# Window attention: the writes of the q and k pieces two slots later on the DMA queue, the layouts of a unit one slot sooner

## The chip, the cores and the metric

The kernel runs on one core of a Trainium2 chip. The metric is the device time of one execution in microseconds, the median of several executions. The core has a matrix engine (TensorE, PE in the profile; its weight loads are PEld), three engines for elementwise work (VectorE or DVE, ScalarE or ACT, GpSimd or POOL), and SyncE (SP). In this kernel SP does nothing but ask for DMA transfers, one after the other, in a fixed order; a request that has to wait holds up all behind it. The row SPq of the profile is that queue.

## The reference: what is computed

The input x has 16 sequences of 512 rows of 128 numbers. The reference is one pre-norm block of attention followed by a product-key expert layer:

```python
x = x + attn(layernorm(x), w_qkv, w_proj)
x = x + ffn(layernorm(x), gamma, beta, w_q, keys, key_in, key_out)
```

Only the attention matters for this change:

```python
q, k, v = split(einsum('btc,oc->bto', x, w_qkv), 3)   # 16 heads of 8 numbers each
attn = einsum('bhqd,bhkd->bhqk', q, k) / sqrt(8)
attn = where(abs(i - j) > 128, -1e9, attn)            # a window of 128 to either side
out  = einsum('bhqk,bhkd->bhqd', softmax(attn), v)
return einsum('btc,oc->bto', out, w_proj)
```

## The kernel before

The program has two stages. The first is the attention for all 16 sequences, with the second norm running beside it; the second stage is the expert layer, which starts when the attention is over. The change touches the first stage alone.

**Units and slots.** A sequence b has 16 heads; four heads together (a group g) make a *unit*, n = 4b + g, so there are 64 units. A unit has four *slots*, u = 0 to 3, one for each block of 128 rows. One loop over s = 4n + u writes out the work of every slot by hand: the scores of unit n + 2 (`greatest`, PE into `s_ps`, then a maximum on DVE into `mx`), the exponentials of unit n (`exponentials`, PE into `e_ps`, then ACT into `pT`, POOL cutting the window), the product with v of two slots earlier (`weigh`), and at most one step of work that is spread over the slots: `preparing` (norm, q, k and v of a sequence ahead), `ending` (the projection of the sequence behind) and `beside` (norms and the weights of the experts). PE and POOL keep the order in which the loop writes their work. The DMA requests are put into one fixed order on SP as well.

**Pieces.** The scores are computed in bf16 at fp32 accuracy: q and k of a sequence are each split into three bf16 pieces whose sum is the fp32 number. POOL does that in `prepare`, in four operations over as many slots: a copy (piece 0), a difference, a copy (piece 1), a difference (piece 2). The tile `pc` holds the three pieces (`qp` or `kp` in the profile).

**Write.** The pieces lie in SBUF with one channel per partition. The score matmul needs pieces and channels of one head together along the partitions, so the tile goes through DRAM: one DMA (L363, 384 KB) writes the three pieces to a DRAM tile `qv` or `kv`. There are 16 writes of q and 16 of k.

**Layout.** `lay(n)` reads them back in the order in which the matmuls want them, into one of six buffers `qst` and `kst`: three DMAs for q (L390), each 96 KB, where one piece is read as three broadcast copies; three for k (L390), 96 KB each; one that clears three rows (L394, `zeros`). The layout of unit n + 4 is asked for in slot 3 of unit n, so it is first read (by the scores) at the beginning of the unit after next:

```python
if u == NQ - 1 and 0 <= n + LAID < NU:
    lay(n + LAID)
```

**The rows of the maximum.** The maximum of every row, negated and split into three pieces as well, is put under q as three more rows of `qst`, so that the matmul of the exponentials subtracts it. POOL splits it in slot 0 of the next unit (`greatest_pieces`), PE transposes it and ACT copies it to `mT` in slot 1 (`greatest_rows`, L440), and three DMAs of 4 KB (L442) move it into `qst`. The first matmul `e_ps` of the following unit needs them.

**What else is asked on SP in this stage:** the load of expert weights (L191, L212), and the transposed second norm of a finished sequence (`xT`, L525, 256 KB).

**The order around the change.** SP has no slots. It asks for the next transfer as soon as that transfer's own conditions hold: its source is written, its destination is read for the last time, and the transfer eight places earlier has landed, for eight completion semaphores are used in turn. In the order before the change, a unit in which a write is asked has on SP: the three mT, the write, the seven of the layout, then the mT of the next unit. The step of `preparing` that asks for a write is in slot 3, after `greatest_rows` of slot 1 and ahead of the layout in the same slot. The q write stands in one unit of a sequence's four and the k write in the next.

In the profile, L168 is the helper for all matmuls of the first stage, L175 for its transposes and L172 for its POOL operations, and L615 is the helper of the second stage.

Of the kernel before, what the change touches and what calls it, by code (L numbers as in the profile page):

```python
# [11 lines left out]
BF16 = mybir.dt.bfloat16  # L12
# [8 lines left out]
P = 128  # L21
# [22 lines left out]
def kernel(  # L44
# [13 lines left out]
    nc = tc.nc  # L58
    B, T, D = x.shape
    NH = 16  # L60
    DK = D // NH
    NQ = T // P
# [18 lines left out]
    for b in range(B):  # L81
        t = keep.tile([P, NQ, D], F32, name=f"x_{b}")
# [59 lines left out]
    def load(b):  # L142
        xts[b] = ahead.tile([P, T], F32, tag="xt", name=f"xt_{b}")
        nc.sync.dma_start(xts[b], xT[b])
# [8 lines left out]
    with ExitStack() as at:  # L153
# [4 lines left out]
        dr = at.enter_context(tc.tile_pool(name="dr", bufs=2, space=bass.MemoryType.DRAM))  # L158
# [7 lines left out]
        def mm(*args, **kw):  # L166

            tc.keep_in_program_order(nc.tensor.matmul(*args, **kw))  # L168

        def pool(op, *args, **kw):  # L170

            tc.keep_in_program_order(getattr(nc.gpsimd, op)(*args, **kw))  # L172
# [92 lines left out]
        NU, NBUF = B * NG, 6  # L265
# [10 lines left out]
        pieced, attns, norms = {}, {}, {}  # L276
# [26 lines left out]
        def ln_stats(bs, name, into):  # L303

            n = len(bs) * NQ
            mv = ln.tile([P, n, 2], F32, tag=f"mv{name}{n}", name=f"mv{name}_{bs[0]}", bufs=3)
            for i in range(n):
                st = ln.tile([P, 6], F32, tag="st", name=f"st{name}_{bs[0]}_{i}", bufs=4)
                nc.vector.bn_stats(st, xs[bs[i // NQ]][:, i % NQ])
                nc.vector.bn_aggr(mv[:, i], st)  # L310
                if i % NQ == NQ - 1:
                    yield
            rstd = ln.tile([P, n], F32, tag=f"rs{name}{n}", name=f"rs{name}_{bs[0]}", bufs=3)
            nc.scalar.activation(rstd[:, 0:n], mv[:, 0:n, 1], AF.Sqrt, bias=eps)
            nc.vector.reciprocal(rstd[:, 0:n], rstd[:, 0:n])
            for i, b in enumerate(bs):
                into[b] = mv[:, i * NQ : i * NQ + NQ], rstd[:, i * NQ : i * NQ + NQ]
            yield

        def normalised_T(b, mv, rstd, dst, tag, then=None):  # L320

            xn = w2.tile([P, NQ, D], F32, tag="xn", name=f"{tag}_{b}")
            for t in range(NQ):

                alone = b == B - 1 if tag == "xi" else b < 2
                what = (xn[:, t], xs[b][:, t], mv[:, t, 0:1], rstd[:, t : t + 1], ALU.subtract, ALU.mult)
                if t % 2 and not alone:
                    pool("tensor_scalar", *what)
                else:
                    nc.vector.tensor_scalar(*what)  # L330
                if t % 2:
                    yield BANK if t == NQ - 1 else None
            ps = ps_m.tile([P, NQ, P], F32, tag="m", name=f"{tag}_ps_{b}")
            for t in range(NQ):
                tr(ps[:, t], xn[:, t], ident)
            nc.scalar.copy(dst, ps.rearrange("p t q -> p (t q)"))
            yield then

        def prepare(b):

            xnT = w2.tile([P, T], F32, tag="xnT", name=f"xnT_{b}")
            yield from normalised_T(b, *norms.pop(b), xnT, "xn", BANK)
            fulls = []
            for what, w in (("q", wqT), ("k", wkT)):
                ps = ps_m.tile([P, T], F32, tag="m", name=f"{what}_ps_{b}")
                mm(ps, lhsT=w, rhs=xnT, start=True, stop=True)
                full = w2.tile([P, T], F32, tag="full", name=f"{what}f_{b}")
                nc.scalar.mul(full, ps, 1.0 / math.sqrt(DK) if what == "q" else 1.0)
                fulls.append((what, full))
                if what == "q":  # L350
                    yield BANK
            for what, full in fulls:
                pc = w2.tile([P, 3, T], BF16, tag="pc", name=f"{what}p_{b}")
                rest = w2.tile([P, T], F32, tag="rest", name=f"rest_{what}_{b}")
                pool("tensor_copy", pc[:, 0], full)
                yield
                pool("tensor_tensor", rest, full, pc[:, 0], ALU.subtract)
                yield
                pool("tensor_copy", pc[:, 1], rest)
                yield  # L360
                pool("tensor_tensor", pc[:, 2], rest, pc[:, 1], ALU.subtract)
                via = dr.tile([3, P, T], BF16, tag=f"{what}v", name=f"{what}v_{b}")
                nc.sync.dma_start(via.rearrange("s c t -> c s t"), pc)  # L363
                pieced[what, b] = via
                yield BANK if what == "k" else None
            va = vaug[b % 3]
            if b < 3:
                nc.gpsimd.memset(va, 0.0)
                nc.gpsimd.memset(va[:, :, :, DK : DK + 1], 1.0)
            v_ps = ps_m.tile([P, NQ, NH, DK], F32, tag="m", name=f"v_ps_{b}")  # L370
            for t in range(NQ):
                mm(
                    v_ps[:, t].rearrange("p h k -> p (h k)"),
                    lhsT=xnT[:, t * P : (t + 1) * P], rhs=wvT, start=True, stop=True,
                )
            nc.scalar.copy(va[:, :, :, 0:DK], v_ps)
            yield

        def lay(n):
# [90 lines left out]
        def weigh(n, u):  # L470

            b, g = divmod(n, NG)
            ts = near(u)
            q0, w = ts[0] * P, len(ts) * P
            pT = probs.pop((n, u))
            if u == 0:
                outs[n] = ps_o.tile([P, T], F32, tag="o", name=f"o_ps_{n}")
            for j in range(4):
                mm(
                    outs[n][32 * j : 32 * j + 32, q0 : q0 + w], lhsT=vaug[b % 3][:, u, 4 * g + j],  # L480
                    rhs=pT[:, j, 0:w], start=u == 0, stop=u == NQ - 1, skip_group_check=True,
                )
            if u == NQ - 1:
                oT = w2.tile([P, T], F32, tag="oT", name=f"oT_{n}")
                nc.scalar.copy(oT, outs[n])
                outs[n] = oT
# [31 lines left out]
        def second_norm(bs):  # L518
            into = {}
            yield from ln_stats(bs, "b", into)  # L520
            for b in bs:
                t = w2.tile([P, T], F32, tag="xiT", name=f"xiT_{b}")
                yield from normalised_T(b, *into[b], t, "xi")
                nc.vector.bn_stats(bn_st[:, b], t)
                nc.sync.dma_start(xT[b], t)  # L525
# [4 lines left out]
        AHEAD, LAID, LATE = 2, 4, 2  # L530
# [8 lines left out]
        for s in range(-2 * NG * NQ, (NU + 1) * NQ):  # L539
            n, u = divmod(s, NQ)  # L540
            b, g = divmod(n, NG)
            if g == NG - 1 and u == 2 and b + 3 < B:
                preparing.rest()
                preparing.add(prepare(b + 3))
            if u == 0 and g == 1 and b == 0:
                beside.add(ln_stats(range(4, B), "a", norms), weights_of_experts())
            if u == 0 and g == 2 and b in groups:
                beside.add(second_norm(groups[b]))
            if u == 0 and g == 2 and b == B - 1:
                load(0)  # L550
                load(1)
            tops_of = greatest(n + AHEAD, u) if 0 <= n + AHEAD < NU else iter(())
            probs_of = exponentials(n, u) if 0 <= n < NU else iter(())
            next(tops_of, None)
            next(probs_of, None)
            next(tops_of, None)
            if 0 <= s - LATE < NU * NQ:
                weigh(*divmod(s - LATE, NQ))
            together(tops_of, probs_of)
            free = True  # L560
            if u == 0 and 0 <= n + AHEAD - 1 < NU:
                greatest_pieces(n + AHEAD - 1)
            if u == 1 and 0 <= n + AHEAD - 1 < NU:
                greatest_rows(n + AHEAD - 1)
                free = False
            if u == 2 and 0 <= n - 1 < NU:
                divide(n - 1)
                free = False
                if n % NG == 0:
                    ending.add(project(n // NG - 1))  # L570
                    ending.go(False)
            for steps in (preparing, ending, beside):
                free = steps.go(free)
            if u == NQ - 1 and 0 <= n + LAID < NU:
                lay(n + LAID)
        beside.add(second_norm([B - 1]))
        ending.rest()
# [366 lines left out]
    for i in range(NB):  # L944
        b, t = divmod(i, NQ)
# [109 lines left out]
```

## Time and profile before

| | |
|---|---|
| median of 3 runs | 1598.37 us (1592.62 to 1599.02) |
| profiled execution, its own time | 1591.23 us |
| span of the profiled execution | 1588.4 us |
| busy: PE, DVE, ACT, POOL | 90%, 86%, 76%, 69% of the span |
| PE busy, 120 to 740 us (attention) | 575 us of 620 us |
| PE busy, 765 to 1588 us (experts) | 753 us of 823 us |
| mean granted clock of PE | 0.987 |
| DMA, q1 (all that SP asks for) | 71.59 MB, 15.3% of 16 engines over the span |

How to read it: the page gives for every engine the time it was busy, and for every idle stretch which event ended it (its releaser). A line such as "PE s_ps L168 <- DMA qst<-mT" is PE standing idle ahead of a matmul that writes `s_ps`, until a transfer from `mT` into `qst` landed. Lines with SPq tell how long SP held a request, and for what. "issue" is time in which an engine waited for nothing that the profile shows. The chain of waits follows the work that ended last back from the end, so that it shows what a shorter wait could shorten. Ends of matmuls are modelled, so short gaps on PE are less certain than the long ones.

### The profile page before, as it was taken

To read this page: it belongs to the slowest core of one execution; us is meant where nothing else is said; L and a number is where in the kernel's file an instruction comes from. 1 tells how busy PE (TensorE), PEld (TensorE's weight loads), DVE (VectorE), ACT (ScalarE), POOL (GpSimd) and SP (SyncE) were. 2 spreads that over 40 slices of the span, in tenths; PEclk is the share of its full clock that TensorE was granted. 3 is DMA by queue.
4 is the path that set the end of the run, shared out by engine and by line. 5 is a ranking of instruction groups with operands and counts; after the bars stand their busy time and mean duration, and the time that the engine had idled before them with its cause. 6 is when DMAs were issued, how large, how long until landed. Compare 5 with 4: busy or idle time off the path is not lost.

```text
span 1588.4 us, 49415 instructions
## 1 busy us (share of the span) xinstructions
PE 1430.3 (90%) x16880; PEld 837.5 (53%) x16880; DVE 1363.5 (86%) x7998; ACT 1213.0 (76%) x2593; POOL 1092.8 (69%) x1706
## 2 busy tenths in 40 slices
PE   4899999999999999987689999999999999999998
PEld 1344444444444444433356666666666666666666
DVE  6787778888878887885799999999999999999994
ACT  1476676677767776677688988898988988988973
POOL 8465666666666676655377777777777777777785
PEclk9999999999999999999799999999999999999998
DMA  6233232222222233221000000000000000000000
GB/s 181 66 106 94 86 88 80 74 81 76 71 77 86 83 96 92 75 62 40 34 9 3 16 9 15 16 9 16 9 16 16 9 16 9 16 15 9 9 2 22
DMA packets 53579, 75.00 MB, mean 47 GB/s; under 512 B 5840, under 2 KB 39888, under 8 KB 53200
## 3 DMA queue, kind: packets, MB, share of 16 engines
q1 hardware_dynamic: 52496, 71.59, 15.3%
q8 instruction: 133, 2.18, 0.6%
q14 instruction: 118, 0.97, 0.2%
q10 hardware_dynamic: 832, 0.26, 0.1%
HBM read 49.28 MB, written 20.97 MB: 44 GB/s over the span
## 4 chain that ended last, share of the span: by engine, by line
PE 40%; DVE 21%; ACT 17%; DMA 9%; POOL 8%; issue 3%; SPq 2%; DVEq 0%; ACTq 0%; POOLq 0%
PE o_ps L168 7%; PE s_ps L168 7%; ACT L615 5%; PE e_ps L168 5%; DMA qst<-qv 5%; DVE idx L615 4%; PE off_ps L615 4%; PE dn_ps L615 4%; DMA qst<-mT 4%; DVE row L615 4%; PE up_ps L615 3%; DVE masked L415 3%; ACT gel L615 2%; ACT pT L457 2%; PE sim_ps L615 2%
## 5 line engine op out<-in xcount | busy, mean ns | idle before, releaser
L415 DVE CUSTOM_DVE_ANT_0 masked<-s_ps,band 128x384 bf16<-128x384 f32 (+1 forms) x1024 | 498.5, 487 | 140.4 <-PE s_ps L168 35.5
L457 ACT ACTIVATE pT<-e_ps 128x384 f32<-128x384 f32 (+1 forms) x1024 | 390.6, 436 | 172.8 <-PE e_ps L168 168.1
L172 POOL TENSOR_SCALAR_AFFINE_SELECT pT<-pT 128x512 f32<-128x512 f32 x384 | 237.8, 635 | 238.8 <-ACT pT L457 238.5
L168 PE MATMUL s_ps<-kst,qst 128*128 128x384 bf16 (+1 forms) x1024 | 313.9, 308 | 45.1 <-DVE mx L415 13.1
L615 POOL TENSOR_TENSOR cols<-mine,wT 64x512 f32<-64x512 bf16 x256 | 269.4, 1052 | 39.9 <-DVE mine L615 14.5
L615 PEld LDWEIGHTS w_ps<-cols,row 128*64 128x64 f32 x8192 | 246.8, 138 | 52.8 <-POOL cols L615 48.6
L615 PE MATMUL w_ps<-cols,row 128*64 128x32 f32 x8192 | 256.4, 223 | 9.8 <-POOL cols L615 9.6
L615 POOL TENSOR_TENSOR g<-g,gel 128x512 f32<-128x512 f32 x128 | 163.5, 1277 | 124.1 <-ACT g L615 124.1
L168 PE MATMUL e_ps<-qst,kst 128*128 128x384 bf16 (+1 forms) x1024 | 225.8, 302 | 12.0 <-DMA qst<-mT 7.8
L168 PEld LDWEIGHTS <-qst 128*128 128x128 bf16 x1024 | 100.3, 98 | 216.9 <-issue 155.9
L168 PE MATMUL o_ps<-pT,vaug 128*32 128x384 f32 (+1 forms) x2048 | 192.4, 448 | 0.4 <-POOL pT L172 0.3
L615 DVE FIND_INDEX8 idx<-top,sim 128x8 uint32<-128x32 f32 x1024 | 166.2, 185 | 0.0
L615 ACT ACTIVATE row<-off_p,one 128x512 f32<-128x512 bf16 x256 | 165.7, 747 | 0.0
L615 ACT ACT_TABLE_LOAD x122 | 156.5, 1283 | 2.2
L615 DVE TENSOR_TENSOR row<-x_ps,nums_p 128x1024 f32<-128x1024 f32 x128 | 150.1, 1214 | 0.0
L615 ACT ACTIVATE off_p<-off_ps 128x512 bf16<-128x512 f32 x256 | 133.4, 603 | 20.9 <-PE off_ps L615 20.9
L615 PE MATMUL up_ps<-g,key_out_sb 64*128 64x256 f32 (+2 forms) x1152 | 146.3, 380 | 0.0
L168 PEld LDWEIGHTS <-kst 128*128 128x128 bf16 x1024 | 97.8, 98 | 53.4 <-issue 19.5
L615 PE MATMUL dn_ps<-xt,key_inT 128*64 128x256 f32 x1024 | 125.3, 388 | 0.0
L615 PE MATMUL off_ps<-p_bf,ident_bf 128*128 128x512 bf16 x256 | 99.9, 390 | 19.9 <-ACT p_bf L615 19.5
L615 DVE MAX8 top<-sim 128x8 f32<-128x32 f32 x1024 | 106.8, 177 | 4.6 <-ACT sim L615 4.6
L615 DVE FIND_INDEX8 place<-best,cand 128x8 uint32<-128x64 f32 x512 | 101.0, 218 | 0.0
(145 smaller groups left out, 2343.4 us busy)
## 6 DMA issues: line engine op xcount, KB each, us to landing
qst<-qv SPq DMA_DIRECT2D x192, 96.0 KB
kst<-kv SPq DMA_DIRECT2D x192, 96.0 KB
qv<-qp SPq DMA_DIRECT2D x16, 384.0 KB
kv<-kp SPq DMA_DIRECT2D x16, 384.0 KB
x<-in_L_attn_x_dram SPq DMA_DIRECT2D x16, 256.0 KB
xT<-xiT SPq DMA_DIRECT2D x16, 256.0 KB
xt<-xT SPq DMA_DIRECT2D x16, 256.0 KB
out_dram<-o_sb SPq DMA_DIRECT2D x16, 256.0 KB
```

What stands on the lines that cost most here:

```text
L168: tc.keep_in_program_order(nc.tensor.matmul(*args, **kw))
L172: tc.keep_in_program_order(getattr(nc.gpsimd, op)(*args, **kw))
L415: nc.vector.tensor_tensor_reduce(masked[:, 0:w], s, band.rearrange("p u k -> p (u k)")[:, from_u : from_u + w], 1.0, LOWEST, ALU.add, ALU. ...
L457: nc.scalar.activation(pT[:, h, 0:w], e_ps[:, 0:w], AF.Exp)
L615: return lambda *args, **kw: tc.keep_in_program_order(op(*args, **kw))
```

## The change

Two things are moved, and nothing else.

The request that writes the q pieces is no longer made behind the last of the four POOL operations on q, but two slots later, behind the third POOL operation on k. The request for the k pieces is made one step of `preparing` after the v matmuls, in a new last step, which is two slots later as well. Until a write is asked for, `pieced` holds the SBUF tile; from then on the DRAM tile. The layout of unit n + 4 is asked for in slot 2 of unit n in place of slot 3.

```diff
@@ prepare(b)
+            def write(what):
+
+                via = dr.tile([3, P, T], BF16, tag=f"{what}v", name=f"{what}v_{b}")
+                nc.sync.dma_start(via.rearrange("s c t -> c s t"), pieced[what, b])
+                pieced[what, b] = via
+
             for what, full in fulls:
...
                 pool("tensor_copy", pc[:, 1], rest)
+                if what == "k":
+                    write("q")
                 yield
                 pool("tensor_tensor", pc[:, 2], rest, pc[:, 1], ALU.subtract)
-                via = dr.tile([3, P, T], BF16, tag=f"{what}v", name=f"{what}v_{b}")
-                nc.sync.dma_start(via.rearrange("s c t -> c s t"), pc)
-                pieced[what, b] = via
+                pieced[what, b] = pc
                 yield BANK if what == "k" else None
...
             nc.scalar.copy(va[:, :, :, 0:DK], v_ps)
+            yield
+            write("k")
             yield
@@ the loop over slots
-            if u == NQ - 1 and 0 <= n + LAID < NU:
+            if u == NQ - 2 and 0 <= n + LAID < NU:
                 lay(n + LAID)
```

In the order on SP this gives, in the steady part of the stage: the three mT, the write, the layout, and so on, as before; but a write stands behind the mT of the unit after the one in which it stood. The transfers of `xT` and of the expert weights that were asked between a write and a layout stand behind the layout. The orders of PE, DVE and ACT are the same in both kernels.

## The prediction

> **What bounds the kernel now.** I read the page first: PE is busy 90% of the span, and the chain that ended last gives DMA 9%: "DMA qst<-qv" 5%, "DMA qst<-mT" 4%. Both belong to the attention stage (roughly 40 to 755 us); the expert stage after it has no line of the change. So the question is what PE loses to these two transfers. The waits of PE between 120 and 740 us answer it; columns: us in total, times, longest.
>
> ```profile
> PE s_ps L168 <- DMA qst<-mT: 12.8, 13, 2.5
> PE e_ps L168 <- DMA qst<-mT: 7.8, 17, 1.3
> PE s_ps L168 <- DMA qst<-zeros: 4.1, 6, 1.8
> ```
>
> That is 24.7 us of PE standing still for rows of the maximum (mT) or the last piece of a layout (zeros). Next, why these land late: the waits of the SP queue, which asks for every transfer in turn.
>
> ```profile
> SPq L363 <- POOL qp L172: 60.9, 16, 5.2
> SPq L363 <- POOL kp L172: 43.4, 16, 4.0
> SPq L442 <- DMA qst<-qv: 12.0, 21, 1.1
> ```
>
> Each of the 32 writes (L363) holds the queue until POOL has made the last piece, 3.3 us on average (104.3/32); behind it stand the layouts and the next mT. The timeline of SP over three units shows it: after the mT of 549.03 the queue sits from 550.94 to 555.00, the layout goes out only then, and the mT of 559.89 is asked the moment the layout is through. Where no write is asked (581.90), the layout follows its mT at once.
>
> ```profile
> 549.03 1.91 SPq L442 DMA_DIRECT2D qst<-mT  x3
> 555.00 0.39 SPq L363 DMA_DIRECT2D qv<-qp  x1
> 555.44 2.21 SPq L390 DMA_DIRECT2D qst<-qv  x3
> 559.89 2.48 SPq L442 DMA_DIRECT2D qst<-mT  x3
> ...
> 581.90 1.91 SPq L442 DMA_DIRECT2D qst<-mT  x3
> 583.86 2.22 SPq L390 DMA_DIRECT2D qst<-qv  x3
> ```
>
> The chain of waits through one such place runs from POOL over the write and the layout into the mT, and then into PE (start, length):
>
> ```profile
> 521.10 1.13 POOL kp L172
> 522.25 0.39 SPq L363
> 524.58 5.75 DMA qst<-qv
> 530.35 2.27 DMA qst<-mT
> 532.71 0.38 PE e_ps L168 x2
> ```
>
> Last, the size of it: four units of one batch, cut at the copies of mT. Columns: length, then busy time of PE, PEld, DVE, ACT, POOL, granted clock, DMA share, GB/s.
>
> ```profile
> 548.45:558.47 10.02, 9.99 (x86) 5.35 (x84) 8.55 (x37) 7.41 (x21) 8.09 (x15) 1.00 0.16 49
> 558.47:570.20 11.73, 10.56 (x86) 5.30 (x84) 10.32 (x45) 7.88 (x22) 8.38 (x15) 1.00 0.33 106
> 570.20:581.30 11.10, 9.51 (x81) 4.75 (x79) 9.80 (x39) 8.01 (x21) 7.70 (x15) 1.00 0.40 120
> 581.30:591.86 10.56, 10.41 (x78) 4.73 (x78) 8.37 (x37) 7.84 (x21) 6.40 (x14) 1.00 0.26 73
> ```
>
> Call them A, B, C and D. PE is idle 0.03, 1.17, 1.59 and 0.15 us: only the two units behind a write lose anything. The same cut over the thirteen batches from 124.78 us gives an idle time of 15.8 us in the B units and 19.4 us in the C units, 35.2 in 26 units (1.35 each); it holds the 24.7 named above and the small gaps around them. Three C units (136.22, 438.38, 613.42) ran at a granted clock of 0.87 right after stalls of 1.8, 2.5 and 1.2 us: PE is busy 11.22, 10.82 and 11.32 there, against 9.9, 9.1 and 9.5 in C units like them. That is 4.8 us more that hang on the stalls.
>
> **The change part by part.** No instruction is added, removed or given another shape. The orders of PE, DVE and ACT stay as they were; POOL's differs in its first 60 instructions alone, where a half of xn comes ahead of the last k piece in place of a memset (about 0.8 us by half of the 1.59 us for two, against 0.95): startup 0, between -1 and +1 us, for the first score matmul waits on that k piece (10.24 us idle before it at 37.16). What moves is on SP.
>
> *The writes.* Before: mT, write, layout. After: mT, layout (no write any more in that gap), mT, write, layout: the same place, one unit later. The pieces of the q write at 511.59 would be asked for behind the mT of 516.46, when they have been ready for over 5 us. The 104.3 us of SP waiting go, and with them the delay of layout and mT. POOL's queue is not touched. A write costs SP 0.39 us, ahead of the layout as now.
>
> *The layouts.* Seven requests (three q, three k, one zeros; 2.21 + 1.25 + 0.77 us and gaps, 4.35 in all). In a unit without a write they leave as soon as SP has sent the mT, so an earlier slot gives them nothing; it puts them ahead of the loads of expert weights, and of anything else asked at the slot. One line has one answer: 0 by itself.
>
> *What the move puts at risk.* Eight transfers can be open: a request waits for the one eight before it. The third mT therefore waits for the second q layout, or for the third where an xT lies between. From the chain above: the second q layout lands at 530.33, 8.1 us after its write began at 522.25. In the new order the write begins some 2.0 us behind its mT (1.91 and a gap), so that layout lands 10.1 us after the first mT, and the next third mT goes out at 10.4 + 1.2 = 11.6 us: 1.5 us of margin, 0.75 with an xT (one more q request, 0.75). That is thin, and covers it all; if it is gone, the wait of today is back in the same place. The k write is laid out one unit after it is written instead of two: about 11 us against 18 (522.25 to 540.26); in the startup the layout of k followed its write within 2.8 us (27.86 to 30.63), so this costs 0.
>
> *What is late next.* Units without a trouble idle 0.15 (D); the two early units with writes and no stall (82.95 and 93.49) idle 0.75 and 0.67. I put 0.5 us of idle time on each of the 26 units, nearer to the early ones as these have the same work on SP: 35.2 - 13 = 22.2 us saved; the bounds are 35.2 - 18.2 = 17 and 35.2 - 3.9 = 31. Of the slow-clock stretches two of three go: 3 us (0 to 4.8). D now follows a write, a layout and an xT: I charge 0.2 us in each of 13: -2.6 (0 to -6). Sum 22.2 + 3 - 2.6 = 22.6. The profiled execution took 1591.23 us (span 1588.4, 2.8 around it): 1569. The median shown is 7.1 us above it, so I forecast 1575.
>
> **Rivals.**
> *The transfer engines stay full (1582).* A unit without a write has a DMA share of 0.16 over 10.02 us: 25.7 engine-us of 16 engines. The q layouts are written as three broadcast copies; if the whole layout lay on three engines they would be busy 8.6 us of it, and a write (0.33 x 16 x 11.73 - 25.7 = 36 engine-us, 2.3 per engine) makes 10.8: longer than a unit of 10.5, and mT would land some 0.3 us late in B and C. Saved: 35.2 - 26 x 0.8 + 2 = 16. For it: the 5.75 us that a q layout of 96 KB takes to land. Against it: D carries a layout and an xT and idles 0.15. The Trainium skill, "DMA: Bandwidth & Descriptors", Rules for kernel authors, says that a leading broadcast of c copies confines a transfer to at most c engines, which speaks against the change: the order in which SP asks would then matter less than what is queued on those engines. By the page's figure of about 27 GiB/s per engine one q layout is, as an estimate, 1.1 us on three engines; by the trace it lands after 5.75 us, so the trace neither confirms nor excludes it.
>
> *Nothing to be measured (1594).* DVE is busy 10.3 us of B and 9.8 of C in the batches with a second norm, and it could take over as the bound: B then stays at 10.9 or so. That holds in five of thirteen batches; elsewhere DVE has 8 to 9.2. It takes away 5 us at most by itself, so it needs half of the rival above too. To this case also belongs that the mT is late for another reason (ACT copies it late), against which stand A and D.
>
> *Slower (1612).* The margin of 0.75 to 1.5 us above is eaten: if writes and layouts, now asked back to back right behind mT, land 2 us later than the 5.75 of today, the third mT is 1.25 us late in B and C, and in D, which is quiet today: 39 units x 1.25 = 49 us against 35 lost now, +14. It decides at 0.9 us late in 39 units, thus at about 7.4 us for a q layout. Against it: writes and layouts were asked back to back before, at the same length of queue.
>
> **How the numbers follow.** Forecast, stalls mostly gone (1562 to 1584): 0.70. Engines full (1577 to 1590): 0.15. Nothing to be measured (1588 to 1600): 0.09. Slower (1607 to 1620): 0.06. A measurement of this kernel tells about 0.5%, 8 us, from no change. Faster by more than that (under 1590) takes the first case and most of the second, 0.84; within it 0.10; slower 0.06. The range of 8 in 10 runs from 1561, just under the first case, to 1590, the far end of the second; the likeliest one's own is 1562 to 1584.
>
> **What would show it.** In the waits of SP, L363 on POOL falls from 104 us to under 10, and L442 on "DMA qst<-qv" nearly vanishes. On the timeline each write stands directly behind an mT, and the layout 0.4 us later. PE's waits for mT and zeros between 120 and 740 us fall from 24.7 to under 8. B units come to 10.5 to 11.0 us, C to 9.7 to 10.4; A and D stay at 10.0 and 10.6; the 0.87 clock is seen in at most one C unit. If B and C stay above 11 while L363 no longer waits, the transfer engines were the cause; if D grows beyond 11, the slower rival's mechanism is there. The expert stage stays at 833 us.

## The result and the profile after

The changed kernel takes 1573.86 us (median of 6 runs, 1570.27 to 1578.66); the kernel before, with three more runs, 1593.99 us (1587.25 to 1599.02). The ratio is 0.9872, 95% interval 0.9848 to 0.9896: faster by 1.3%. The forecast was 1575 us, 84% for faster.

First the waits of SP in the changed kernel (L356 is the write, L399 the layout, L451 the three mT):

```profile
SPq L451 <- ACT pT L466: 259.5, 63, 7.9
...
SPq L356 <- POOL qp L172: 5.2, 1, 5.2
SPq L399 <- DMA qst<-qv: 3.8, 5, 1.5
SPq L356 <- POOL kp L172: 3.7, 1, 3.7
```

A write now waits for its pieces on POOL twice in the whole run (8.9 us in place of 104.3; both in the startup, before 120 us, where the kernel before has 16.4), and no mT waits for an earlier layout. The time that SP spends waiting has not gone; it has moved to where SP should wait: L451 stands for ACT at each mT, 63 times in place of 52, with nothing late behind it.

The timeline of SP over two units with a write:

```profile
545.27 2.00 SPq L451 DMA_DIRECT2D qst<-mT  x3
547.37 0.39 SPq L356 DMA_DIRECT2D qv<-qp  x1
547.81 2.23 SPq L399 DMA_DIRECT2D qst<-qv  x3
...
556.46 1.93 SPq L451 DMA_DIRECT2D qst<-mT  x3
558.49 0.39 SPq L356 DMA_DIRECT2D kv<-kp  x1
558.92 2.22 SPq L399 DMA_DIRECT2D qst<-qv  x3
```

The write goes out 0.1 us behind its mT, where it stood 4 us behind before, and the layout 0.44 us after it.

The waits of PE between 120 and 740 us (us in total, times, longest):

```profile
PE s_ps L168 <- DVE mx L424: 15.4, 62, 0.6
PE e_ps L168 <- ACT pT L466: 4.7, 5, 1.3
PE mT_ps L175 <- POOL mp L172: 4.6, 13, 1.1
...
PE s_ps L168 <- DMA qv<-qp: 0.3, 2, 0.2
```

The 24.7 us for mT and zeros are gone entirely. In their place PE waits longer for DVE: 15.4 us, against 8.0 before in the same window. In the chain that ended last over the whole span, DMA falls from 9% to 1%. The share of DVE does not rise there (21% before, 18% here), but it is 29% in a second execution of the same kernel, so it can't carry a reading:

```profile
PE 54%; DVE 18%; ACT 17%; POOL 7%; issue 4%; DMA 1%; SPq 0%; DVEq 0%; POOLq 0%; ACTq 0%
```

Last, the four units of the same batch (length, then busy time of PE, PEld, DVE, ACT, POOL, clock, DMA share, GB/s):

```profile
534.38:544.69 10.31, 9.98 (x86) 5.35 (x84) 8.49 (x37) 7.41 (x21) 8.10 (x15) 1.00 0.21 59
544.69:555.88 11.19, 10.54 (x86) 5.34 (x84) 9.99 (x43) 7.78 (x22) 8.38 (x15) 1.00 0.34 114
555.88:566.71 10.83, 9.89 (x81) 4.81 (x79) 9.42 (x39) 7.89 (x21) 7.95 (x15) 1.00 0.35 116
566.71:577.81 11.10, 10.81 (x78) 4.76 (x78) 8.87 (x37) 7.88 (x22) 6.13 (x13) 1.00 0.21 63
```

B falls from 11.73 to 11.19, C from 11.10 to 10.83, and D rises from 10.56 to 11.10. Over the whole steady part, from the eighth copy of mT on, the means are:

| unit | length before | after | PE idle before, in all | after |
|---|---|---|---|---|
| A (12) | 10.02 | 10.00 | 0.5 | 0.5 |
| B (13) | 11.66 | 11.10 | 15.8 | 8.1 |
| C (13) | 11.26 | 10.16 | 19.4 | 8.9 |
| D (12) | 10.49 | 10.81 | 1.6 | 2.8 |

In sum 14.3 us from C and 7.3 from B, less 3.9 in D. The last copy of mT, near the end of the attention, comes at 715.33 us in place of 733.11: 17.8 us sooner. The profiled execution took 1578.66 us (span 1575.9), 12.6 less than the one before, since the rest of the span, from that copy to the end, was 860.6 us long in place of 855.3. A second execution of the same kernel had the copy at 714.34 and a rest of 858.1; its B units average 10.99 us, since the one at a granted clock of 0.87 that stands in the B row above (13.27 us, shown below) took 11.72 us there at full clock.

### The profile page after: what moved, and what is told of

It reads as the page before. It is cut to its first block, busy times and chain, and to the rows that moved or that the text cites. A ratio compares the mean times of both kernels' runs of the same rounds, so it can differ in the third digit from the quotient of the medians.

```text
span 1575.9 us, 49416 instructions
## 1 busy us (share of the span) xinstructions
PE 1436.0 (91%) x16880; PEld 842.0 (53%) x16880; DVE 1361.4 (86%) x7998; ACT 1211.9 (77%) x2593; POOL 1092.7 (69%) x1706
## 4 chain that ended last, share of the span: by engine, by line
PE 54%; DVE 18%; ACT 17%; POOL 7%; issue 4%; DMA 1%; SPq 0%; DVEq 0%; POOLq 0%; ACTq 0%
PE s_ps L168 10%; PE o_ps L168 10%; PE e_ps L168 6%; ACT L624 6%; DVE masked L424 5%; PE off_ps L624 5%; PE dn_ps L624 4%; PE up_ps L624 4%; DVE idx L624 3%; POOL cols L624 3%; PE sim_ps L624 3%; ACT gel L624 3%; DVE row L624 2%; PE w_ps L624 2%; PE t_ps L175 1%
## 5 line engine op out<-in xcount | busy, mean ns | idle before, releaser
L424 DVE CUSTOM_DVE_ANT_0 masked<-s_ps,band 128x384 bf16<-128x384 f32 (+1 forms) x1024 | 498.5, 487 | 125.5 <-PE s_ps L168 16.5
L168 PE MATMUL s_ps<-kst,qst 128*128 128x384 bf16 (+1 forms) x1024 | 313.0, 307 | 35.4 <-DVE mx L424 20.7
L624 PEld LDWEIGHTS up_ps<-g,key_out_sb 64*128 64x128 f32 x1152 | 94.8, 188 | 12.3
```

Of the source, the lines that this page charges most:

```text
L424: nc.vector.tensor_tensor_reduce(masked[:, 0:w], s, band.rearrange("p u k -> p (u k)")[:, from_u : from_u + w], 1.0, LOWEST, ALU.add, ALU. ...
L624: return lambda *args, **kw: tc.keep_in_program_order(op(*args, **kw))
```

## The experiments

Each kernel was timed on the same chip as the kernel before; ratios are to the kernel before, with 95% intervals.

**The writes alone.** The changed kernel with the layouts back in slot 3.

```diff
-            if u == NQ - 2 and 0 <= n + LAID < NU:
+            if u == NQ - 1 and 0 <= n + LAID < NU:
                 lay(n + LAID)
```

> The change with its layouts left in slot 3: only the writes go two slots later. SP then asks in the same order as the changed kernel, but for one write in the startup and five loads of expert weights that stay ahead of a layout. Theory (SP is held behind a write whose pieces are not ready, and layout and mT stand behind it): the whole gain, a ratio to the kernel before of 0.985 to 0.990, and L356 waiting for POOL under 15 us in all. Rival (the earlier slot of the layouts is what makes them land in time): about half of the gain or less, 0.993 to 1.000.

Measured: 0.989 (0.9863 to 0.9918); last copy of mT at 715.02 us, where the changed kernel has 715.33. L356 stands for pieces 11.1 us in all (k 5.8, q 5.3), all of it before 120 us, and PE has no wait for mT or zeros. The writes alone bring the whole gain; with the writes moved, the slot of the layouts does nothing that can be measured.

**The layouts alone.** The kernel before with the layouts in slot 2.

```diff
-            if u == NQ - 1 and 0 <= n + LAID < NU:
+            if u == NQ - 2 and 0 <= n + LAID < NU:
                 lay(n + LAID)
```

> The kernel before with only the layouts one slot sooner: on SP the layout then stands ahead of the write, which stays in slot 3 and still waits for POOL. Theory (what costs is the layout that stands behind the waiting write): the gain without any change to the writes, ratio 0.985 to 0.990, while L363 goes on waiting for POOL for some 50 to 110 us in all; PE's waits for mT and zeros between 120 and 740 us fall from 24.7 to under 8 us. Rival (the 104 us of SP waiting cost by themselves, or a write close ahead of mT delays it): a ratio of 0.995 to 1.005, and PE goes on waiting for mT.

Measured: 0.9872 (0.9848 to 0.9896); last copy of mT at 713.21 us. The layouts alone bring the whole gain, too. The timeline of SP in this kernel shows how; the write (L363) stands behind the layout, at the end of the unit:

```profile
543.24 1.99 SPq L442 DMA_DIRECT2D qst<-mT  x3
545.28 2.21 SPq L390 DMA_DIRECT2D qst<-qv  x3
547.53 1.25 SPq L390 DMA_DIRECT2D kst<-kv  x3
548.83 0.78 SPq L394 DMA_DIRECT2D qst<-zeros  x1
549.91 0.39 SPq L363 DMA_DIRECT2D kv<-kp  x1
...
554.43 1.91 SPq L442 DMA_DIRECT2D qst<-mT  x3
```

The writes still wait for POOL in the run as a whole, though far less than the 50 to 110 us that I had put down:

```profile
SPq L363 <- POOL kp L172: 12.3, 14, 3.7
SPq L363 <- POOL qp L172: 9.3, 3, 5.3
```

Of these 21.6 us, 16.5 lie in the startup, where the kernel before has 16.4. Between 120 and 740 us the kernel before has

```profile
SPq L363 <- POOL qp L172: 51.6, 13, 4.3
SPq L363 <- POOL kp L172: 36.2, 13, 4.0
```

and this one

```profile
SPq L363 <- POOL kp L172: 5.1, 11, 1.7
```

The earlier layout thus takes nearly all of the waiting away as well: SP spends 4.3 us on the layout, and by then the pieces are ready or nearly so. This run therefore does not set the waiting of SP apart from what stands behind it. That the wait costs through the layout and the mT behind it is what the chain of waits says, and no run here holds SP as long with nothing behind it. PE's waits for mT and zeros are gone here as well.

**The writes asked by POOL.** The kernel before, with the request on another engine and the bytes moving when they moved before.

```diff
-                nc.sync.dma_start(via.rearrange("s c t -> c s t"), pc)
+                nc.gpsimd.dma_start(via.rearrange("s c t -> c s t"), pc)
```

> The kernel before with the 32 writes asked by POOL itself, at the same place in its program, instead of by SP: SP is never held by a piece, the writes go out when the pieces are ready as before, and the layouts follow their mT. Theory (holding SP is the cause): PE's waits for mT and zeros go as in the changed kernel, the gain less what asking costs POOL (32 requests of 1 to 2 us on an engine that is busy 70% of the stage): ratio 0.986 to 0.995. Rival (the time at which the bytes of the writes move is the cause, next to the mT): these move when they moved before, so PE goes on waiting for mT and the ratio is 0.997 to 1.005.

Measured: 0.9916 (0.9891 to 0.9942); last copy of mT at 719.01 us. PE's waits of this kernel between 120 and 740 us hold 1.2 us for a q layout and 0.2 us for mT, and its weight loads wait 2.0 us for mT and zeros together, where they waited 32.2 before; what rises is the wait for POOL:

```profile
PE s_ps L168 <- DVE mx L415: 14.4, 64, 0.4
PE mT_ps L175 <- POOL mp L172: 12.2, 33, 1.1
PE e_ps L168 <- ACT pT L457: 4.9, 5, 1.6
PE s_ps L168 <- DMA qst<-qv: 1.2, 1, 1.2
```

A request keeps POOL for 0.87 us (the one at 544.73), by this some 28 us for all 32, and the pieces of the maximum come later by it: 12.2 us of PE's time against 4.6 in the changed kernel, and A grows from 10.00 to 10.27 us. The bytes of the writes move at the old time, without harm. Holding SP was the cause, and not the place of the writes' bytes.

**More writes.** The changed kernel with every write made three times, and then five times; the added ones go to scratch that nothing reads.

```diff
                 nc.sync.dma_start(via.rearrange("s c t -> c s t"), pieced[what, b])
+                for i in range(2):     # 4 in the second kernel
+                    idle = dr.tile([3, P, T], BF16, tag=f"{what}i{i}", name=f"{what}i{i}_{b}")
+                    nc.sync.dma_start(idle.rearrange("s c t -> c s t"), pieced[what, b])
```

> The changed kernel with every write asked three times, twice into scratch DRAM tiles that nothing reads: 768 KB and two requests of 0.39 us more on SP in each of the two units of a sequence that have a write. It tells how much room the transfer engines have. Theory (the order of SP was the cause, the transfer engines have room of about 0.8 to 1.5 us in a unit): two more writes of about 2 us each eat it, so the third mT comes 2 to 4 us late in two or three units of a sequence; ratio to the kernel before 0.995 to 1.02, to the changed kernel 1.01 to 1.03, with PE waiting for mT again. If the room is larger than I worked out (a write moves in about 1.5 us and layouts end early): no more than 0.5% above the changed kernel, 0.987 to 0.992.

> The changed kernel with every write asked five times, four times into scratch DRAM. With three it cost 7.5 us up to the end of the attention stage, 5.4 of it in the startup. Theory (the transfers had more room than I worked out, and three writes just use it up: PE waits 10.6 us for mT there): two more of about 1.5 us each now come late in full, 2 to 3 us in each of 24 units: ratio to the kernel before 1.01 to 1.04, PE's wait for mT and zeros between 120 and 740 us 40 to 80 us. Rival (there is still room, what three cost was the startup alone): 0.994 to 1.000.

Measured with three: 0.9926 (0.9898 to 0.9955), which is 1.0055 of the changed kernel: between my two cases. The last copy of mT comes at 722.88 us, 7.5 later, but 5.4 of these are there before the steady part begins (3.4 in one C unit at a granted clock of 0.87); the 49 units from the eighth copy on take 518.4 us in place of 516.3 (515.0 in the second execution of the changed kernel). Measured with five: 1.03 (1.027 to 1.0331); the 49 units take 563.8 us, 47.5 more. PE's waits between 120 and 740 us with three writes, the rows on transfers:

```profile
PE e_ps L168 <- DMA qst<-mT: 2.7, 5, 1.0
...
PEld L168 <- DMA qst<-mT: 7.9, 13, 1.2
PEld L168 <- DMA qst<-zeros: 0.6, 1, 0.6
```

and with five:

```profile
PE s_ps L168 <- DMA qst<-zeros: 15.1, 12, 2.0
PE e_ps L168 <- DMA qst<-mT: 13.8, 22, 1.1
...
PE s_ps L168 <- DMA qst<-mT: 8.4, 9, 1.5
```

Two added writes use up the room between one mT and the next, and two more fall on PE's path: C goes from 10.16 to 12.23 and D from 10.81 to 12.95 us, while B, at 10.98, is not touched. Idle time of PE is 35.4 us of that growth; the rest goes with the clock, for ten of these C and D units show a granted clock of 0.86 to 0.89. PE's three rows make 37.3 us, a little under the 40 to 80 that I expected. So the transfers can become the bound, but only above some three times the writes that this kernel has. Two things are not set apart here: the bytes of the added writes, and their requests, 1.6 us of SP for four. SP's own rows with five writes have mT waiting for an earlier q layout to land 43 times, 31.5 us in all.

**What is left.** B and C still idle 0.65 us each. PE's wait for mx on DVE points to the score maxima; three kernels try that.

```diff
# one more of four normalisations of a sequence on POOL in place of DVE
-                if t % 2 and not alone:
+                if (t % 2 or t == 0) and not alone:
# all four
+                if not alone:
# four PSUM buffers for scores, two for exponentials, the norms as they were
-        ps_s = at.enter_context(tc.tile_pool(name="ps_s", bufs=3, space=PSUM))
-        ps_e = at.enter_context(tc.tile_pool(name="ps_e", bufs=3, space=PSUM))
+        ps_s = at.enter_context(tc.tile_pool(name="ps_s", bufs=4, space=PSUM))
+        ps_e = at.enter_context(tc.tile_pool(name="ps_e", bufs=2, space=PSUM))
```

> The changed kernel with one more of the four normalisations of a sequence (first block of both norms, sequences that share the work) on POOL instead of DVE: 0.3 to 0.67 us less on DVE in each place, 0.8 us more on POOL. Theory (what is left of PE's idle time in the two units of a sequence with writes, 17 us in 26 units, is DVE being late with the score maxima): PE's wait for mx between 120 and 740 us falls from 15.4 to under 11 us, 2 to 6 us gained on the changed kernel, ratio to the kernel before 0.982 to 0.987. Rival (POOL, with 0.8 us more in each such place, makes the pieces of the maximum or the window late): PE's wait for mp on POOL rises above the 4.6 us of the changed kernel by as much, ratio 0.986 to 0.995.

> The changed kernel with all four normalisations of a sequence on POOL (two in the changed kernel, three in the run before this). Theory (PE's idle time left in B and C is DVE behind on the score maxima): B falls again by about the 0.2 us a unit that the third block gave (11.10 to 10.87), PE's wait for mx falls below 13.4 us, the attention ends 1 to 4 us before the 712.8 us of the run with three; ratio to the kernel before 0.981 to 0.987. Rival (POOL is now what comes late): waits for mp and for the window's pT rise, the attention ends at 714 to 722 us, ratio 0.986 to 0.992.

> The changed kernel with four PSUM buffers for the scores and two for the exponentials, in place of three and three. Theory (PE stands for the score buffer that DVE has not read yet): the wait for mx falls from 15.4 to under 6 us; but ACT gets its exponentials through two buffers, and if that is as tight the wait of PE for pT rises from 4.7 us by 10 or more. Ratio to the kernel before 0.980 to 0.987 if DVE was what is left, 0.99 to 1.02 if two buffers starve ACT; I expect the second.

> The changed kernel once more, beside the run above on the same chip, so that the two can be set against each other: ratio to the kernel before 0.985 to 0.990 on every theory.

The row of PE's wait for mx with three normalisations on POOL:

```profile
PE s_ps L168 <- DVE mx L424: 13.4, 60, 0.4
```

with all four, with the wait for POOL that comes with it:

```profile
PE s_ps L168 <- DVE mx L424: 9.7, 47, 0.3
...
PE xn_ps L175 <- POOL xn L172: 4.1, 10, 0.4
```

and with four score buffers:

```profile
PE e_ps L168 <- ACT pT L466: 6.1, 6, 2.0
PE s_ps L168 <- DVE mx L424: 6.0, 24, 0.5
...
PE a_ps L175 <- DVE attn L508: 4.3, 11, 0.8
```

| kernel | ratio | last copy of mT | A, B, C, D |
|---|---|---|---|
| changed | 0.9872 (0.9848 to 0.9896) | 715.33 | 10.00, 11.10, 10.16, 10.81 |
| changed, again | 0.9888 (0.9866 to 0.991) | 714.34 | 10.00, 10.99, 10.16, 10.82 |
| three norms on POOL | 0.9849 (0.9821 to 0.9877) | 712.77 | 10.04, 10.87, 10.10, 10.82 |
| four norms on POOL | 0.9884 (0.9862 to 0.9906) | 711.38 | 10.00, 10.85, 10.54, 10.32 |
| four score buffers | 0.9928 (0.9906 to 0.995) | 717.05 | 10.42, 10.46, 10.43, 10.92 |

With each of the three the wait for mx falls, and B with it, which supports DVE as what is late in B. Against the second execution, which has no slow B unit, B falls by 0.12 and 0.14 us with the norms and by 0.53 with a fourth score buffer. But what is taken there comes back elsewhere. With all four norms on POOL, D becomes 0.5 us shorter and C 0.4 us longer, where PE waits for xn. With four score buffers A and C become 0.4 and 0.3 us longer. I had expected a long wait for pT, and the row of that wait grew by 1.4 us only. Another row grew: PE stands 4.3 us at the transposes into `a_ps` for `attn`, which DVE makes (0.8 us in the changed kernel), and 3.4 of it lie in the A units. So DVE comes late with other work there; why it does with these buffers is not shown.

Against what was set down beforehand: the wait for mx with three norms on POOL came to 13.4 us and not under 11; with all four the row and the end of the attention came as the theory had them, but the ratio, 0.9884, lies outside its 0.981 to 0.987. The gain of the two kernels with norms in the attention (1.6 to 3.9 us against the two executions of the changed kernel) is less than what the times resolve: three norms on POOL is the lowest of all, at 0.9849, but its interval lies over that of the changed kernel.

## Why the prediction was right

**The mechanism, step by step.** The chain that was read from the profile (POOL, write, layout, mT, PE) is the cause: take the hold away by moving the writes, or by moving the layouts ahead of the writes, or by giving the writes to another engine, and PE's waits for mT and zeros go every time, but for 0.2 us of PE and 2.0 us of its weight loads in the last. The Trainium skill, "DMA: Bandwidth & Descriptors", Anatomy of one DMA — SWDGE (gpsimd) path, says that DMA engines do not wait on semaphores and that every such wait happens on the issuing sequencer; the trace agrees for the requests of SP, with 104.3 us of SP standing at the writes and the layouts behind them late.

**The sum.** Forecast from the profiled execution: 22.6 us. Measured in the profiles: 17.8 us up to the last copy of mT (18.8 in the second execution). By terms:

- Idle time of B and C: forecast 35.2 - 13 = 22.2 saved, measured 35.2 - 17.0 = 18.2. The idle time that stays is 0.65 us a unit and not 0.5; it lies with the 0.67 to 0.75 of the two early units that I had named as the nearer end.
- D: charged 0.2 us in each unit, 2.6; measured 0.32 in each of 12, 3.9. The reason I gave (the transfers behind a write) is not borne out: D has no wait for a transfer. DVE is busy 8.87 us in the D unit shown, against 8.37 before, and with all norms on POOL D falls by 0.5 us; the work of DVE that used to fit into the stalls of B and C comes later. That last link is argued: in the D unit shown PE's named wait for DVE is 0.2 us in both kernels, its idle time goes from 0.15 to 0.29 us, and the same 78 matmuls keep it busy 10.81 us in place of 10.41.
- The slow clock: 3 us for two of three stretches. In the changed kernel no C unit runs at 0.87; one B unit does, 13.27 us long, in which ACT is busy 10.08 us, with two table loads of 1.28 us around the square root of the second norm (416.96 and 418.60); they stand in the kernel before as well, in a unit at full clock. By the busy time of PE 4.8 us are gone and 1.6 came new (11.64 us against 10.09 in the second execution), 3.2 net. That the slow stretches hang on the stalls is supported by the kernel with five writes: all ten slow units from the eighth copy on are C or D units in which PE idles 1.7 to 2.9 us, and the eight executions of kernels without these stalls have two slow units there between them, the one below and one with four score buffers, both with ACT busy some 10 us. A stall need not bring it on: the B unit at 341.86 of the kernel before idles 2.4 us at full clock.

```profile
414.28:427.55 13.27, 11.64 (x82) 5.37 (x80) 9.74 (x45) 10.08 (x24) 7.58 (x14) 0.87 0.26 79
```

- Startup: 0 forecast; the eighth copy of mT comes at 124.82 us, before at 124.78.

Together 18.2 - 3.9 + 3.2 = 17.5, close to the 17.8 measured.

**The level.** That the forecast lies within 1.2 us of the time is partly luck: two errors offset each other. The median of the kernel before over six runs is 1593.99 us, 4.4 below the three runs that were shown, so the saving by medians is 20.1 us and not 23.4; and 1575 was reached because the saving was put too high by nearly as much (3.3). In the profiled execution the expert stage did not stay as it was: the rest of the span was 5.3 us longer. The eleven profiles of this study have a rest of 855.3 to 864.5 us, and it goes with the clock granted in it: 855.3 to 858.4 us in the six with 0.98, 860.6 to 864.5 in the five with 0.97, with the same 11852 matmuls. The two executions of the changed kernel lie on either side, so the change does not set it by itself.

**The step that was wrong.** "The layouts ... 0 by itself": I looked at the units without a write, where the layout leaves at once in any case, and did not go through the units with a write, where the earlier slot takes the layout past the write that holds the queue. There it does by itself all that the whole change does. The two halves of the change are two ways to the same end, and either would have been enough.

**The margin.** Worked out as 0.75 to 1.5 us between a layout's landing and the next mT; in fact two more writes fit nearly free. Two terms of that working were too large. One is the 5.75 us in which a q layout landed: it was measured where the layout was asked late and the next mT was asked right behind it, and no mT waits for a layout in the new order; how soon a layout lands there no row shows. The other is the size of a write, 36 engine-us, 2.3 us of every transfer engine. It was read off a B unit, which holds parts of two layouts (asked at 555.44 and 566.15) beside its write. The pages of the changed kernel and of those with three and five writes have, in packets, MB and share of 16 engines over the span:

```profile
q1 hardware_dynamic: 52496, 71.59, 15.6%
...
q1 hardware_dynamic: 78096, 96.76, 20.0%
...
q1 hardware_dynamic: 103696, 121.93, 23.6%
```

This is about 18 engine-us for each of the 64 and 128 added writes, 1.1 us of every engine: half of what I took. With it the first rival's own sum is 8.6 + 1.1 = 9.7 us, below the 10.5 of a unit. "The transfer engines stay full" is refuted for this kernel, and so is "slower" at its price; with five writes PE waits for transfers again, at 1.03. The Trainium skill's rule on a leading broadcast ("DMA: Bandwidth & Descriptors", Rules for kernel authors), which spoke for full engines, is neither confirmed nor refuted: no row here shows on how many engines a layout lies.

**DVE** as the bound was a rival at 0.09 together with others; the rows point to it as what limits the gain: 15.4 us of PE's waiting in place of 8.0, and B at 11.10 on average (10.99 in the second execution) and 11.19 in the batches with a second norm, at or above the end of the 10.5 to 11.0 that I gave.

## What to carry to other kernels

A queue that asks for transfers in order should not have a request whose data is not there yet in front of one that somebody waits for; look for it in the waits of the queue, and then ask what stands behind the waiting request, and not only how long it waits. Here 87.8 us of such waiting between 120 and 740 us cost some 18 us of the attention. In the startup it cost nothing that shows: 16.4 us of it before the change and 8.9 after it leave the eighth copy of mT where it was, at 124.78 and 124.82 us. When two edits are made together, go through each alone in every kind of unit: an edit that does nothing in the quiet ones may do everything in the others.

## What was not expected of the hardware

The transfers had more room than the landing times suggested: writing 1152 KB in place of 384 KB in two of four units lengthened the steady part by 2.1 us of 516 (3.4 against the second execution), and 1920 KB by 47.5 us. Somewhere between these two the room is used up.

Giving a request to POOL costs that engine 0.87 us, against 0.39 us on SP. Here the attention ended 3.7 us later by it (719.01 against 715.33); the ratios, 0.9916 against 0.9872, have intervals that touch.

The rest of the span, which is the expert stage but for its first few per cent, took 855.3 to 858.4 us in the profiles in which the granted clock was 0.98 there and 860.6 to 864.5 where it was 0.97, and one and the same kernel is found in both. The kernel with four score buffers is 0.6% slower than the changed one by the ratios; only 1.7 us of that lie in the attention of the profiles, and its rest of 864.5 us, the longest of all, is one of those at 0.97. What sets the clock there stays open.
